# A fourth tile on GpSimd, exponentials taken from PSUM ahead of a top-16 search, and a product in two halves

## The chip, the cores and the metric

The kernel runs on one core of one Trainium2 chip. The metric is the device time of one launch in microseconds (us). The engines are named as in the profile: PE is TensorE's matrix multiply and PEld its weight load, DVE is VectorE, ACT is ScalarE, POOL is GpSimd, and SP issues most of the DMAs.

## The reference

Four transformer blocks, one after the other, act on x of 128 batches x 64 tokens x 128 channels, with a context of the same shape and a conditioning vector for each batch. All is f32. Each block has layer norms, whose scale and shift come from the conditioning, attentions with 16 heads of 8 channels, and from the second block on an MLP. The third block holds the part that matters here: a cross attention that keeps only the 16 greatest of 64 scores in each row, and takes the softmax over these.

```python
def _ln(x):
    m = x.mean(-1, keepdims=True)
    v = jnp.mean((x - m) ** 2, axis=-1, keepdims=True)
    return (x - m) * jax.lax.rsqrt(v + EPS)
...
scores = jnp.einsum('bqhd,bkhd->bhqk', q, k) / jnp.sqrt(jnp.float32(D))
top_s, top_i = jax.lax.top_k(scores, TOPK)          # TOPK = 16 of 64
attn = jax.nn.softmax(top_s, axis=-1)
vg = jnp.take_along_axis(v_bh[:, :, None, :, :], top_i[..., None], axis=3)
o = jnp.einsum('bhqk,bhqkd->bqhd', attn, vg).reshape(B, L, C)
```

There are 128 x 16 x 64 = 131,072 such rows of scores.

## The kernel before

**Chunks and lanes.** The 128 batches are cut into 16 chunks of 8 batches, which is 512 tokens: four tiles (NT = 4) of 128 tokens x 128 channels. Eight lanes work on eight chunks at once; each lane takes its next chunk when the former is nearly written out. A chunk passes through all four blocks: seven attentions, three MLPs, and twelve normal forms (ten of x, two of the context).

**The planner.** No operation is written in the order in which it is executed. Each one is recorded by `op` (L179) with an engine, a cost in ns, the tiles that it writes and reads, and a closure that issues its instructions. `Plan.run` (L347) then picks, step by step, the operation that can start earliest by these costs, over a window of 80 operations in each lane. The costs are jittered by up to 1% (`near`, L324), from the numbers in LUCK, one for each 350 steps; another LUCK gives another order. Operations with `port=True` are kept apart in the plan between DVE and POOL (L232), and a POOL operation of this kind is made to wait for the last such DVE instruction where that is near (L294). Tiles come from pools: 30 of "some" (128 x 512 f32 in SBUF), three "mm" banks, two "ps" and one "po" in PSUM.

**The normal form.** `moments` (L699) takes the sums on DVE, `normal` (L714) takes the root on POOL (L719, L720) and then, on DVE, four tensor_scalar instructions (L727), one for each tile, of which each subtracts a mean and multiplies by the root. `flip` (L688) turns the four tiles on PE (L694) into PSUM, and `modulate` (L735) multiplies by the scale (DVE, L738) and adds the shift (POOL, L739).

**Attention.** Ordinary rows go through `weigh` (L808): scores on PE (L819), exponentials on ACT straight out of PSUM (L830), the weighted sums on PE (L949), a copy (L959), a spill to DRAM (L960), the sums and their reciprocal (L977, L984), and a product on POOL (L994). The searched rows of the third block go through `weigh_rows` (L836), with queries on the partitions. Each call has two halves of 8 score rows x 64. A half is copied from PSUM by ACT (L867). On DVE, for each of the 8 rows, MAX8 finds the 8 greatest (L887), MATCH_REPLACE8 takes them out (L889), and a second MAX8 finds the next 8 (L891). One scalar_tensor_tensor (L902) then makes a mask of all scores that are not less than the sixteenth, and sums the mask into `counts`. ACT takes the exponential of the copy in place (L909), POOL multiplies it by the mask (L917), and PE turns the result (L925) for the weighted sums.

**The check at the end and the safe network.** The counts of all chunks add up in `acc[2]` (L1012), and the reciprocals and sums of the softmaxes in `acc[0]` and `acc[1]` (L1007, L1008). After the last chunk three comparisons are made, and the third of them asks for exactly sixteen in every row:

```python
    nc.vector.tensor_scalar(ok[:, 8 * NH :], acc[2], float(8 * TOPK * nchunk), None, ALU.is_equal)
...
    with tc.If(rows_ok < P):
        network(1, True)
```

`network(1, True)` is the whole network once more, with one lane, fewer buffers and `safe` set: every attention then takes `weigh_rows`, the ordinary ones subtract the row's maximum first (L870, L871), and the search takes its 16 out one by one with a second MATCH_REPLACE8, so that equal scores are told apart.

**The MLPs.** `mlp_out` (L1064) sums four products for each of the four token tiles into one PSUM bank, 16 matrix products recorded as one PE operation (L1072), and `residual` follows on DVE and POOL.

Of the kernel before, what the change touches and what calls it, by code (L numbers as in the profile page):

```python
# [10 lines left out]
AF = mybir.ActivationFunctionType  # L11
# [10 lines left out]
NT = T // P  # L22
# [2 lines left out]
COPIES = 8  # L25
MLP = 512
LANES = 8
NJ = MLP // P
LUCK = (
    47423, 97277, 61821, 98454, 87219, 72030, 46625, 79421, 30261, 36474, 64224,  # L30
    16425, 63569, 65745, 68055, 16097, 89257, 63092, 89779, 79691, 72039,
)
NSOME = 30
NQBD, NPROB, NVAL = 3, 8, 4
SCALE = 1.0 / math.sqrt(HD)
# [64 lines left out]
PE, DVE, ACT, POOL, SP, LATER = "PE", "DVE", "ACT", "POOL", "SP", "LATER"  # L100
# [31 lines left out]
class Plan:  # L132
# [43 lines left out]
        t.real, t.taken = real, True  # L176
        return t

    def op(self, engine, cost, outs, ins, give, latency=0.0, bulk=False, table=None, small=0, within=False, port=False, moves=None, rate=1.0, code=4):  # L179
        tiles = list(dict.fromkeys([*outs, *ins]))  # L180
        needs = {}
        for t in tiles:
            if t.writer is not None:
                needs[t.writer] = True
        for t in outs:
            needs.update(dict.fromkeys(t.readers))
        o = Operation(engine, cost, latency, tiles, needs, give, bulk, table, small, within, port)
        o.moves, o.rate, o.code = moves, rate, small or code
        self.count += 1
        o.serial = self.count  # L190
        o.ev = 0 if engine == PE or any(t.kind in self.PSUM for t in tiles) else 1
        for t in outs:
            t.writer, t.readers = o, []
        for t in ins:
            if t not in outs:
                t.readers.append(o)
        for t in tiles:
            t.ops.append(o)
        self.ops.append(o)
# [180 lines left out]
def kernel(ctx: ExitStack, tc: tile.TileContext, ins: dict, out: bass.AP, nchunk: int = NCHUNK):  # L380
    nc = tc.nc
# [55 lines left out]
    def prepare(plan, ready, pieces, all_of_it, vblocks, queries, pool, spills):  # L437
# [7 lines left out]
        def clear(kind, cost, give):  # L445
            t = plan.tile(lambda: None, kind)
            _, t.slot = plan.free[kind].pop()
            t.taken = True
            op(POOL, cost, [t], [], lambda: give(t.slot))
# [193 lines left out]
    def lane(n, plan, work, safe, acc, pieces, vblocks, queries, pool, spills):  # L643
# [4 lines left out]
        op = plan.op  # L648

        def of(*names):  # L650

            return [t for name in names for t in pieces.get(name, ())]

        def sb(shape, tag, bufs=1):
            name = f"{tag}{n}"
            return plan.tile(lambda: work.tile(shape, F32, tag=name, name=name, bufs=bufs), name, bufs)

        def mm(name):
            return plan.tile(lambda: mm_tile(name), "mm")

        def shared(shape, tag):

            return plan.tile(lambda: work.tile(shape, F32, tag=tag, name=tag, bufs=plan.size[tag]), tag)

        def some(shape):


            def make():
                a = pool[t.slot]
                return a.rearrange("p (a b) -> p a b", a=shape[1]) if len(shape) == 3 else (  # L670
                    a.rearrange("p (a b c) -> p a b c", a=shape[1], b=shape[2]) if len(shape) == 4 else a
                )

            t = plan.tile(make, "some")
            return t
# [9 lines left out]
            ), 3130, moves=(893, 538))  # L685
            return t

        def flip(x, name):  # L688

            p = mm(name)  # L690

            def turn():
                for t in range(NT):
                    nc.tensor.transpose(p()[:, t * P : (t + 1) * P], x()[:, t, :], ident)  # L694

            op(PE, 510, [p], [x], turn, rate=0.75, code=2 * NT)
            return p

        def moments(x, tag="parts"):  # L699
# [14 lines left out]
        def normal(x, mv, eps):  # L714

            rstd = sb([P, NT], "rstd", 2)

            def root():
                nc.gpsimd.tensor_scalar(rstd().unsqueeze(2), mv()[:, :, 2:3], 1.0 / D, eps, ALU.mult, ALU.add)  # L719
                nc.gpsimd.tensor_tensor(rstd(), rstd(), minus_half, ALU.pow)  # L720

            op(POOL, 1295, [rstd], [mv], root)
            xn = some([P, NT, D])

            def norm():
                for t in range(NT):
                    nc.vector.tensor_scalar(  # L727
                        xn()[:, t, :], x()[:, t, :], mv()[:, t, 1:2], rstd()[:, t : t + 1], ALU.subtract, ALU.mult
                    )

            op(DVE, 1180, [xn], [x, mv, rstd], norm, port=True)

            return flip(xn, "pn")

        def modulate(h, pn, key, scale, shift, c):  # L735
            made = of((key, scale), (key, shift))
# [16 lines left out]
        def attention(hq, hkv, wq, bq, wk, wv, made, topk=False):  # L753
# [82 lines left out]
            def weigh_rows(i, prs):  # L836

                quad, gp = divmod(i, 2)
                psc = plan.tile(lambda: ps_s.tile([P, 2, 2, 2, 2, S], F32, tag="ps", name="ps"), "ps")
# [20 lines left out]
                for half in range(2):  # L860
                    ex = some([P, 8, S])

                    def s8(half=half):
                        return psc().rearrange("p g u k b s -> p (g u k b) s")[:, 8 * half : 8 * half + 8]

                    if topk:
                        op(ACT, 585, [ex], [psc], lambda ex=ex, s8=s8: nc.scalar.copy(ex(), s8()))  # L867
                    else:
                        mx = sb([P, 8], "mx", 2)
                        op(DVE, 680, [mx], [psc], lambda mx=mx, s8=s8: nc.vector.tensor_reduce(mx(), s8(), AX.X, ALU.max))  # L870
                        op(DVE, 680, [ex], [psc, mx], lambda ex=ex, mx=mx, s8=s8: nc.vector.tensor_tensor(  # L871
                            ex(), s8(), mx().unsqueeze(2).to_broadcast([P, 8, S]), ALU.subtract
                        ))
                    exs.append(ex)
# [31 lines left out]
                            ), port=True)  # L906
                        ws.append(w)
                for half, ex in enumerate(exs):
                    op(ACT, 570, [ex], [ex], lambda ex=ex: nc.scalar.activation(ex(), ex(), AF.Exp, scale=SCALE), table="exp")  # L909
                    if topk:  # L910
                        w = ws[half]
                        if safe:
                            op(DVE, 690, [ex], [ex, w], lambda ex=ex, w=w: nc.vector.scalar_tensor_tensor(
                                ex(), w(), GONE, ex(), ALU.is_equal, ALU.mult
                            ))
                        else:
                            op(POOL, 1255, [ex], [ex, w], lambda ex=ex, w=w: nc.gpsimd.tensor_tensor(  # L917
                                ex(), ex(), w(), ALU.mult
                            ), port=True)
# [120 lines left out]
        def residual(py, x, gate, c, behind):  # L1040
            if isinstance(gate, str):
                op(DVE, 670, [x], [x, py], lambda: nc.vector.tensor_tensor(x(), v3(py()), x(), ALU.add))
            else:
                g = by_token(gate, 0, c, [behind])
                y = some([P, NT, D])
                op(DVE, 650, [y], [py, g], lambda: nc.vector.tensor_tensor(y(), v3(py()), g(), ALU.mult))  # L1046
                op(POOL, 1255, [x], [x, y], lambda: nc.gpsimd.tensor_tensor(x(), x(), y(), ALU.add), port=True)  # L1047
# [16 lines left out]
        def mlp_out(gs, w2, x, gate, c):  # L1064

            py = mm("py")

            def sum_up():
                for t in range(NT):
                    cols = slice(t * P, (t + 1) * P)  # L1070
                    for j in range(NJ):
                        nc.tensor.matmul(  # L1072
                            py()[:, cols], lhsT=gs[j // 2]()[:, j % 2, cols], rhs=W[w2][:, j, :], start=(j == 0), stop=(j == NJ - 1)
                        )

            op(PE, 3610, [py], [*gs, *of(w2)], sum_up, code=4 * NT * NJ)
            residual(py, x, gate, c, gs[1])

        def product(w, j, h, name, *takes):
# [6 lines left out]
        def gelu_mlp(h, w1, b1, w2, x, gate, c):  # L1086
            gs = [shared([P, NJ // 2, T], "prob") for _ in range(2)]

            def part(j):
                ph = product(w1, j, h, "ph", *([] if j else gs))  # L1090
                op(ACT, 690, [gs[j // 2]], [ph, *of("biases")], lambda: nc.scalar.activation(
                    gs[j // 2]()[:, j % 2, :], ph(), AF.Gelu_apprx_tanh, bias=bvec(b1, j)
                ), table="gelu")

            for j in range(NJ):
                part(j)
            mlp_out(gs, w2, x, gate, c)

        def swiglu_mlp(h, w1, b1, w2, x, gate, c):

            gs = [shared([P, NJ // 2, T], "prob") for _ in range(2)]

# [110 lines left out]
    def network(lanes, safe, acc=None):  # L1213
        def warm(tile, ns):
# [4 lines left out]
            while columns > 0:  # L1219
# [4 lines left out]
        slots = {"mm": 3, "ps": 2, "po": 1, "qbd": 1 if safe else NQBD, "prob": 2 if safe else NPROB,  # L1224
                 "values": 1 if safe else NVAL, "some": 10 if safe else NSOME, "spill": 1 if safe else LANES, "turned": 1 if safe else LANES}

# [32 lines left out]
    for a in acc:  # L1259
        nc.gpsimd.memset(a, 0.0)  # L1260
    network(LANES, False, acc)

# [41 lines left out]
```

## Time and profile before

| | |
|---|---|
| time, median of 3 runs | 1746.65 us (1745.8 to 1761.59) |
| the profiled execution | 1752.81 us, of which the span is 1751.0 |
| instructions in the span | 74746 |
| mean granted PE clock | 0.979 |
| busy: PE, DVE, ACT, POOL | 93%, 71%, 73%, 64% |
| normal form on DVE (L727) | 640 + 128 tiles, 262.4 us |
| searched halves: copies (L867), exponentials (L909) | 128 each, 69.7 and 80.1 us |
| search on DVE (L887, L889, L891) | 1024 rows |
| second products of the MLPs (L1072) | 3 x 512 PE instructions, 183.7 us |

The span goes from the first to the last instruction; the profiled execution's own time is 1.8 us longer. A row of the groups gives the line in the code, the engine, the operation, what is written and read with shapes, the count, then busy us and the mean ns of one, and last the idle time of the engine ahead of it with what ended it. Busy shares are averages over the span; a table by windows of 100 us shows which engine is full where.

### The profile page before, as it was taken

How to read it: one execution, taken by the hardware profiler on the slowest of the kernel's cores; microseconds unless marked ns; L12 is line 12 of the kernel's file. 1: busy time of each engine (PE TensorE's matmuls, PEld its weight loads, DVE VectorE, ACT ScalarE, POOL GpSimd, SP SyncE). 2: the span in 40 equal slices, each digit the busy share in tenths (PEclk: the TensorE clock that was granted, in tenths of full speed). 3: DMA queues.
4: the chain of work that ended last, by engine and by line, in shares of the span. 5: the costliest groups of instructions: out<-in, count | busy, mean ns of one | idle time of the engine just before them, and what ended most of it. 6: DMA issues, size and time to landing. Idle time of an engine off the chain costs nothing. (4 is left out here: it accounts for less than half of the span.)

```text
span 1751.0 us, 74746 instructions
## 1 busy us (share of the span) xinstructions
PE 1624.2 (93%) x30425; PEld 1138.2 (65%) x30425; DVE 1248.4 (71%) x6009; ACT 1272.1 (73%) x1806; POOL 1117.3 (64%) x1306
## 2 busy tenths in 40 slices
PE   8977999988899999999998999999998999999998
PEld 5655667666566566766766666677676756666665
DVE  7532545699998976694578379399989899985323
ACT  3745777867587686788687859879887668686762
POOL 8642656666566757675766485586868566666444
PEclk9988999999999999999999999999999899999999
DMA  7576655543334456545654645755454325356343
GB/s 215 164 231 178 189 169 160 158 120 112 92 118 137 115 150 193 147 137 151 171 161 129 184 130 143 211 147 158 125 175 128 98 77 177 108 153 187 118 144 99
DMA packets 296821, 260.86 MB, mean 149 GB/s; under 512 B 53196, under 2 KB 216212, under 8 KB 296468
## 3 DMA queue, kind: packets, MB, share of 16 engines
q1 hardware_dynamic: 296468, 255.99, 50.2%
q8 instruction: 242, 3.96, 1.0%
q14 instruction: 111, 0.91, 0.2%
HBM read 154.83 MB, written 79.04 MB: 134 GB/s over the span
## 5 line engine op out<-in xcount | busy, mean ns | idle before, releaser
L830 ACT ACTIVATE prob<-ps 128x1024 f32<-128x1024 f32 x384 | 376.5, 1025 | 115.1 <-PE ps L819 112.7
L949 PEld LDWEIGHTS po<-prob,vbuf 128*32 128x32 f32 x14336 | 216.1, 111 | 89.1 <-issue 41.0
L949 PE MATMUL po<-prob,vbuf 128*32 128x64 f32 x14336 | 255.9, 223 | 9.6 <-issue 5.1
L727 DVE TENSOR_SCALAR some<-x,parts,rstd 128x128 f32<-128x128 f32 x640 | 212.4, 393 | 65.0 <-POOL rstd L720 64.8
L819 PE MATMUL ps<-qbd,some 32*64 32x256 f32 x6144 | 226.8, 393 | 18.8 <-DMA qbd<-some 14.1
L917 POOL TENSOR_TENSOR some<-some,some 128x512 f32<-128x512 f32 x128 | 163.6, 1286 | 102.7 <-ACT some L909 66.8
L720 POOL TENSOR_TENSOR rstd<-rstd,minus_half 128x4 f32<-128x4 f32 x192 | 199.0, 1037 | 16.0
L889 DVE MATCH_REPLACE8 some<-m,some 128x64 f32<-128x64 f32 x1024 | 206.4, 209 | 0.3 <-issue 0.3
L1047 POOL TENSOR_TENSOR x<-x,some 128x512 f32<-128x512 f32 x112 | 142.8, 1278 | 81.4 <-DVE some L1046 51.2
L994 POOL TENSOR_TENSOR some<-some,some 128x512 f32<-128x512 f32 x112 | 143.4, 1281 | 80.1 <-DMA some<-spillrec 20.9
L959 ACT COPY some<-po 128x512 f32<-128x512 f32 x224 | 132.6, 592 | 77.9 <-PE po L949 64.9
L887 DVE MAX8 m<-some 128x8 f32<-128x64 f32 x1024 | 172.1, 209 | 15.9 <-ACT some L867 15.9
L891 DVE MAX8 m<-some 128x8 f32<-128x64 f32 x1024 | 176.9, 214 | 0.0
L819 PEld LDWEIGHTS ps<-qbd,some 32*64 32x64 f32 x6144 | 119.7, 133 | 83.8 <-issue 41.0
L792 ACT COPY vbuf<-pv 64x512 f32<-64x512 f32 x224 | 154.2, 688 | 27.4 <-PE pv L785 25.3
L739 POOL TENSOR_TENSOR some<-some,mod_L 128x512 f32<-128x512 f32 x112 | 116.7, 1044 | 84.3 <-DVE some L738 62.5
L1038 POOL TENSOR_TENSOR x<-x,some 128x512 f32<-128x512 f32 x112 | 142.9, 1278 | 42.8 <-DVE some L727 26.5
L1046 DVE TENSOR_TENSOR some<-py,some 128x512 f32<-128x512 f32 x112 | 76.1, 683 | 115.8 <-PE py L1059 63.2
L706 DVE BATCH_NORM_STATS2 parts<-x 128x6 f32<-128x256 f32 x320 | 119.7, 418 | 34.9 <-POOL x L1047 34.0
L694 PE MATMUL pn<-ident,some 128*128 128x128 f32 x768 | 122.0, 283 | 7.2 <-DVE some L727 4.7
L694 PEld LDWEIGHTS pn<-ident,some 128*128 128x128 f32 x768 | 89.2, 142 | 51.1 <-issue 16.7
L763 ACT COPY some<-pk 128x512 f32<-128x512 f32 x112 | 66.3, 593 | 57.4 <-PE pk L761 46.5
(202 smaller groups left out, 3252.4 us busy)
## 6 DMA issues: line engine op xcount, KB each, us to landing
spill<-some SPq DMA_DIRECT2D x224, 256.0 KB, 3.4
some<-gates SPq DMA_DIRECT2D x224, 256.0 KB, 3.7
qbd<-some SPq DMA_DIRECT2D x448, 64.0 KB, 2.4
some<-spill SPq DMA_DIRECT2D x112, 256.0 KB, 4.0
some<-spillrec SPq DMA_DIRECT2D x112, 256.0 KB, 4.5
some<-in_ctx_dram SPq DMA_DIRECT2D x48, 256.0 KB, 5.1
gates<-once SPq DMA_DIRECT2D x7, 1024.0 KB, 7.4
x<-in_x_dram SPq DMA_DIRECT2D x16, 256.0 KB, 4.5
```

What stands on the lines that cost most here:

```text
L694: nc.tensor.transpose(p()[:, t * P : (t + 1) * P], x()[:, t, :], ident)
L720: nc.gpsimd.tensor_tensor(rstd(), rstd(), minus_half, ALU.pow)
L727: nc.vector.tensor_scalar(xn()[:, t, :], x()[:, t, :], mv()[:, t, 1:2], rstd()[:, t : t + 1], ALU.subtract, ALU.mult)
L792: nc.scalar.copy(v4(vbuf())[rows, :, :, 0 : 2 * HD].rearrange("p m h (d b) -> p m h d b", b=2)[:, :, :, :, b], pv()[rows].rearrange("p (m ...
L819: nc.tensor.matmul(pscs[g // 2]()[b * S : (b + 1) * S, g % 2, u].rearrange("p (h q) -> p h q", h=4), lhsT=kT()[rows, cols], rhs=qbd()[rows ...
L830: op(ACT, 975, [pr], [psc], lambda pr=pr, psc=psc: nc.scalar.activation(pr().rearrange("p g u h q -> p (g u h q)"), psc().rearrange("p g u ...
L887: nc.vector.max(m1()[:, j, :], ex()[:, j, :])
L889: nc.vector.match_replace(w()[:, j, :], m1()[:, j, :], ex()[:, j, :], GONE)
L891: nc.vector.max(m2()[:, j, :], w()[:, j, :])
L917: op(POOL, 1255, [ex], [ex, w], lambda ex=ex, w=w: nc.gpsimd.tensor_tensor(ex(), ex(), w(), ALU.mult), port=True)
L949: nc.tensor.matmul(po()[32 * j : 32 * j + 32, g, u], lhsT=vbuf()[:, at : at + 32], rhs=prs[gp]()[:, gi, u, j], start=True, stop=True,)
L994: nc.gpsimd.tensor_tensor(oT().rearrange("p (t b q) -> p b t q", b=2, q=S), oS().rearrange("p (b t q) -> p b t q", b=2, q=S), rb().rearran ...
```

## The change

Three edits, and a new LUCK for the planner.

- In `normal`, DVE makes the first three tiles and POOL the fourth, with a recorded cost of 450 ns. The tile of POOL's result is the same buffer; `beside` keeps the two writers from being ordered one after the other in the plan, and `flip` waits for both. Both have `port=True`.
- In the searched attention of the first network, ACT takes the exponential as it reads PSUM, and the search, the mask and the count work on exponentials. The copy and the exponential in place are gone there. The safe network keeps copying the scores, searching these, and taking exponentials afterwards.
- `mlp_out` records its products as two operations of two token tiles each.

```diff
+ONDVE = 3
...
-    def op(self, engine, cost, outs, ins, give, latency=0.0, bulk=False, table=None, small=0, within=False, port=False, moves=None, rate=1.0, code=4):
-        tiles = list(dict.fromkeys([*outs, *ins]))
+    def op(self, engine, cost, outs, ins, give, latency=0.0, bulk=False, table=None, small=0, within=False, port=False, moves=None, rate=1.0, code=4, beside=()):
+        tiles = list(dict.fromkeys([*outs, *ins, *beside]))
         needs = {}
         for t in tiles:
-            if t.writer is not None:
+            if t.writer is not None and t not in beside:
                 needs[t.writer] = True
...
-            op(PE, 510, [p], [x], turn, rate=0.75, code=2 * NT)
+            op(PE, 510, [p], [x, *rest], turn, rate=0.75, code=2 * NT)
...
-            def norm():
-                for t in range(NT):
-                    nc.vector.tensor_scalar(
+            rest = plan.kept(True)
+
+            def norm(engine, tiles):
+                for t in tiles:
+                    engine.tensor_scalar(
                         xn()[:, t, :], x()[:, t, :], mv()[:, t, 1:2], rstd()[:, t : t + 1], ALU.subtract, ALU.mult
                     )
 
-            op(DVE, 1180, [xn], [x, mv, rstd], norm, port=True)
-
-            return flip(xn, "pn")
+            op(DVE, 885, [xn], [x, mv, rstd], lambda: norm(nc.vector, range(ONDVE)), port=True)
+            op(POOL, 450.0, [rest], [x, mv, rstd], lambda: norm(nc.gpsimd, range(ONDVE, NT)), beside=[xn], port=True)
+
+            return flip(xn, "pn", rest)
...
                     if topk:
-                        op(ACT, 585, [ex], [psc], lambda ex=ex, s8=s8: nc.scalar.copy(ex(), s8()))
+                        if safe:
+                            op(ACT, 585, [ex], [psc], lambda ex=ex, s8=s8: nc.scalar.copy(ex(), s8()))
+                        else:
+                            op(ACT, 585, [ex], [psc], lambda ex=ex, s8=s8: nc.scalar.activation(
+                                ex(), s8(), AF.Exp, scale=SCALE
+                            ), table="exp")
...
                 for half, ex in enumerate(exs):
-                    op(ACT, 570, [ex], [ex], lambda ex=ex: nc.scalar.activation(ex(), ex(), AF.Exp, scale=SCALE), table="exp")
+                    if safe or not topk:
+                        op(ACT, 570, [ex], [ex], lambda ex=ex: nc.scalar.activation(ex(), ex(), AF.Exp, scale=SCALE), table="exp")
...
-            def sum_up():
-                for t in range(NT):
+            def sum_up(half):
+                for t in (2 * half, 2 * half + 1):
...
-            op(PE, 3610, [py], [*gs, *of(w2)], sum_up, code=4 * NT * NJ)
+            for half in range(2):
+                op(PE, 1805, [py], [*gs, *of(w2)], lambda half=half: sum_up(half), code=2 * NT * NJ, within=half > 0)
```

More of the change, by code (lines that the diff above doesn't have):

```diff
@@ L27 @@
 LANES = 8
+ONDVE = 3
 NJ = MLP // P
 LUCK = (
-    47423, 97277, 61821, 98454, 87219, 72030, 46625, 79421, 30261, 36474, 64224,
-    16425, 63569, 65745, 68055, 16097, 89257, 63092, 89779, 79691, 72039,
+    47848, 24402, 28621, 90625, 6804, 13538, 44993, 48557, 31650, 48712, 55050,
+    6092, 66723, 82014, 54051, 14593, 75315, 99856, 95817, 45787, 46198,
 )
@@ L686, in load, with flip @@
             return t
-        def flip(x, name):
+        def flip(x, name, *rest):
             p = mm(name)
```

## The prediction

> **What bounds the kernel now.** I read the page's busy shares first, then the table of 100 us windows, then the groups of instructions by form, then the two lines about the normal form, and last the timeline of the final chunk, where one lane can be followed alone.
>
> ```profile
> PE 1624.2 (93%) x30425; PEld 1138.2 (65%) x30425; DVE 1248.4 (71%) x6009; ACT 1272.1 (73%) x1806; POOL 1117.3 (64%) x1306
> ...
> L727 DVE TENSOR_SCALAR some<-x,parts,rstd 128x128 f32<-128x128 f32 x640 | 212.4, 393 | 65.0 <-POOL rstd L720 64.8
> ...
> L917 POOL TENSOR_TENSOR some<-some,some 128x512 f32<-128x512 f32 x128 | 163.6, 1286 | 102.7 <-ACT some L909 66.8
> ```
>
> TensorE is busy in 93% of the span; nothing that takes work from the other engines can give back more than its idle 127 us, and the start (0 to 200 us: 14 + 18 us idle) and the last 51 us (9 us idle) don't contain the changed search at all. The rest is in the windows where VectorE searches for the sixteen greatest:
>
> ```profile
> 400.00:500.00 100.00, 84.68 (x1616) 56.97 (x1617) 97.00 (x637) 69.99 (x107) 58.45 (x62) 0.97 0.40 116
> 500.00:600.00 100.00, 92.57 (x1730) 64.69 (x1728) 92.33 (x531) 74.10 (x107) 65.98 (x73) 0.97 0.43 124
> ...
> 1200.00:1300.00 100.00, 96.34 (x2038) 68.86 (x2041) 90.56 (x497) 85.98 (x124) 68.55 (x79) 1.00 0.52 154
> ```
>
> The columns are PE, PEld, DVE, ACT, POOL, granted clock, DMA. VectorE at 90% and over is what holds TensorE there; with the windows at 1300 and 1400 TensorE idles 40.5 us in these five. The reader should also see the counts: the search (L887) has 1024 instructions, 16 chunks x 8 halves x 8 rows. The program ran its network **once**. That is a fact about the data, not only about the schedule.
>
> **The change, part by part.** The sums go against the profiled execution (1752.81 us, span 1751.0 and 1.8 around it), which is 6.2 us over the median of the runs shown, 1746.65.
>
> *The fourth tile.* 192 normal forms of four tiles each are 768 instructions, 262.4 us of DVE (212.4 + 50.0). A quarter, 65 us, leaves DVE. POOL has no 128x128 one-source row: from below, its 128x4 form (0.238 us, L719); from above, two sources at 128x64 and 128x512 (0.342 and 1.28 us), which put 128 columns at 0.48 us. I take 0.45 (one source instead of two): 192 x 0.45 = 86 us, POOL from 64% to 69%. In no window does it pass 77% (the most is 72). What stands behind it on POOL's in-order queue is the next chunk's roots, shifts and residual adds.
>
> Here a rule speaks against the word "beside". The trace has one tile at 240 ns at least, 340 as median, 1475 at most, and POOL waiting 26.5 us for it at L1038:
>
> ```profile
> L727 DVE TENSOR_SCALAR some<-x,parts,rstd x640: 240/340/1475, 16.3 to 1731.5; 128x128 f32<-128x128 f32 x160
> ...
>   POOL x L1038: 26.5, 22
>   POOL x L1033: 16.7, 20
>   POOL x L1047: 16.6, 13
> ```
>
> The 1475 is a tile plus about one 1.28 us add of POOL. The Trainium skill (SBUF — State Buffer, section Who interferes with whom) says that VectorE's two-port tensor_scalar and any GpSimd operation hold one shared pair of ports in turn, the loser blocked for the whole instruction. Four tiles undisturbed take 1.11 us in the timeline at 1701.18. If both really ran beside, the form would take max(0.83, 0.45) = 0.83 us, a gain of 0.28; by the rule 0.83 + 0.45 = 1.28, a loss of 0.17. The 1475 makes me take the rule. So the gain isn't a shorter form: it is VectorE's queue, 65 us less over the span, of which five windows of 17.5 hold 19 us.
>
> *Exponentials straight out of PSUM.* In the one pass, 128 copies (L867, 0.594 us) become exponentials and 128 exponentials (L909, 0.638) go. One that reads PSUM costs between the copy's 0.59 and 0.69 (L770, with a bias); I take 0.60. ACT: 128 x (0.594 + 0.638 - 0.60) = 81 us less, 73% to 68%. POOL's product L917 no longer waits for ACT after the search (66.8 us of its idle time); next late is the search itself. The 20 table loads ahead of L909 (25.7 us) move ahead of L867, no gain counted. The cover is TensorE's other lanes; without it the search starts a load (1.28 us) later, 20 times, 26 us.
>
> *Second sums in halves.* The same 32 instructions, 3.57 us in the chain, now twice 1.79 with room for another lane's matmul between. Nothing on TensorE changes; from -5 us (a ready scores group goes 1.8 us earlier, a few dozen times, mostly covered) to +5 (py held longer); I take 0.
>
> Sum for the one pass: up to 19 us from VectorE's windows, perhaps 5 from ACT's (TensorE's weight loads for L949 and L819 wait 25.7 us for the exponentials L830), less 9 for POOL's longer queue (a tenth of its added 86): -15. That gives 1738 on the profiled execution, **1732** against the median.
>
> **What the exponential does to the check.** The kernel keeps every score that is not less than the 16th greatest (L902), counts what it kept, and asks at L1268 for exactly 16 in each row, 8 x 16 x 16 = 2048 per partition and column; one row with 17 makes rows_ok less than 128, and L1276 then runs the whole network again with one lane in the safe form. Before, the compared numbers are raw scores; after, they are exponentials, f32 in a f32 tile. That matters because these scores are small. From the reference's inputs: scaled scores have a standard deviation of 0.052, so their exponentials lie about 1, where f32 steps are 1.19e-7 (0.6e-7 under 1), while a raw score near 0.1 has steps of 0.75e-8. There are 128 x 16 x 64 = 131,072 rows. Gaps of the 16th to the 17th exponential: median 0.0014, but ten rows lie under one step. Rounded to f32, **three rows have the 16th equal to the 17th**; summing 1 - gap/step over the ten rows expects 4.6, and with the scores shifted by 3e-8 to 1e-6 (other orders of rounding) there were 1 to 9 such rows, never none. At four expected, none at all has a chance of e^-4, 2%. Of raw scores the same sum expects 0.1 rows and the reference has none, which agrees with the single pass in the trace.
>
> A second rule bears on this: the Trainium skill (ScalarE: Activation LUTs, section ACT is a hardware spline evaluator) has exp off by up to 165 units in the last place, a smooth cubic on each segment. Smooth means that the rounding step still decides: it shifts which rows tie, not how many. With the rule or with exact exponentials I expect some four rows. No run here shows it.
>
> **The price of a second pass.** It has one lane, so latencies add. Out of the timeline from 1692.89 to 1716: the normal form from moments to shifted h, 6.3 us (1699.01 to 1705.32); queries to first scores 6.0 (1692.89 to 1698.90); scores 1.1; then 8 halves with a maximum and a subtraction on DVE out of PSUM, each as long as L738 (0.68): 10.9; exponential, transposes, copy 2.1; weighted sums and copy 1.9; from the spill through sums, reciprocal, spillrec to the broadcast back 15.7 (1699.65 to 1710.82 and the 4.5 to land); product with rb, projection, two residuals 4.6. Together 49 us. Six such are 294. The searched one has per half four groups at 0.9 us in the timeline, 1.3 with the second replacement, and 0.69: 5.9 x 8 = 47 in place of 10.9, so 85. Three MLPs, each 6.3 + 5.7 + 3.7 + 2.0 = 18, with the second products of the gated one 56. Load and store 7. A chunk is 442 us, and the next one can't begin on x before: 16 x 442 = 7070. With the first pass 1738 + 7070 = 8808, say **8800** us. If a quarter of each chunk overlaps (the context's side, the next gates) it is 7000; if waits in SP's one queue and a slower TensorE clock add 28%, 10800.
>
> **The rivals.** *A, the forecast:* a tie, second pass, 8800 (7000 to 10800). For it: the count of ties and the check in the code. Against: no row of this trace compares exponentials. *B:* every row has exactly 16, one pass, and TensorE's waits behind VectorE shrink: 1732 (1712 to 1755). It is the one on the other side: its place is L1268, its price zero, and it decides if no row ties, or if I read the count wrongly. *C:* one pass, and POOL's tile costs more than it saves: it waits in turn for VectorE's three with all that is queued behind; at 0.17 us on each of 192 forms 33 us if nothing covers it, 1785 - 6 = 1779. It decides where a form is on TensorE's path; the chain has L727 at only 1%, which is against it. *D:* one pass, all of it hidden behind TensorE: 1747.
>
> **How the numbers follow.** A 0.62, B 0.28, C 0.05, D 0.05. The tie count alone would give A more; I hold it down because it rests on the reference's rounding and my reading of the count, neither seen on this chip. A measurement of this kernel tells about 1% from no change. Faster by over 1%: two thirds of B, 0.19. Within 1%: the rest of B and D, 0.14. Slower: A and C, 0.67. The range has to hold A and most of the one-pass cases: 1712 to 10800; A's own stands above.
>
> **What would show it.** The page would have about double the instructions, L867's safe copies and the DVE maximum of L870 present, TensorE busy under a third over the whole, and slices full in the first fifth and thin after. In the first pass: no L909 for the search, DVE's normal form x576, POOL's x192 at 0.35 to 0.50. I am wrong if the span ends near 1740 with 1024 search instructions; then the ties are absent or not counted. A second pass of under 5 ms would make the latency sum wrong, not the mechanism.

## The result: 8747.5 us, and the profile after

The changed kernel takes 8747.5 us (8745.41 to 8749.01, 4 runs) against 1746.61: 4.998 times as long, 95% interval 4.971 to 5.025. The page of the changed kernel says at once what happened. These are its span, its busy shares, and its VectorE, ACT and POOL slices (each slice is 219 us):

```profile
span 8746.0 us, 213897 instructions
...
PE 7265.9 (83%) x89547; PEld 4432.1 (51%) x89547; DVE 3562.6 (41%) x15033; ACT 2997.0 (34%) x4619; POOL 2431.5 (28%) x2734
...
DVE  4796699423242424232424242323242324232423
ACT  5767777522222222222222222222222222222222
POOL 6777787511111111111111111111111111111111
```

There are 213,897 instructions where there were 74,746. Eight slices are full, as before; then 32 thin ones follow, and VectorE's digits rise to 4 about once in two slices, which is one searched attention to each chunk. The second network ran. Its start can be read to the microsecond at the conversion of the count (tile n_ok, L1285):

```profile
L1285 DVE CAST n_ok<-pok x1: 134/134/134, 1737.7 to 1737.7; 1x1 int32<-1x1 f32 x1
```

From there to the end are 8746.0 - 1737.7 = 7008 us. The table of two windows (PE, PEld, DVE, ACT, POOL, clock, DMA share, GB/s) sets the passes side by side:

```profile
0.00:1738.00 1738.00, 1612.32 (x30405) 1124.89 (x30405) 1214.55 (x5817) 1204.93 (x1675) 1268.14 (x1498) 0.98 0.52 150
1738.00:8746.00 7008.00, 5653.59 (x59142) 3307.23 (x59142) 2348.10 (x9216) 1792.06 (x2944) 1163.32 (x1237) 0.91 0.12 36
```

In the second pass DMA falls from 52% to 12%, and ACT and POOL to 26% and 17%. That is one lane whose steps wait for each other. PE looks busy, at 81%. But 3216 of its 5654 us are fillers, matrix products without use that the planner puts into long gaps (L1232); the network's own work is 38% of the second pass. Here are L1232's share of the second window (PE, PEld, clock, DMA share, GB/s), and groups after 1745 us with shapes kept apart:

```profile
1738.00:8746.00 7008.00, 3215.76 (x7430) 1427.23 (x7430) 0.91 0.12 36
...
L1232 PE MATMUL pn<-ident 128*128 128x512 f32 x1264 | 672.8, 678 | 0.0
L1232 PE MATMUL ppt<-ident 128*128 128x512 f32 x1238 | 666.9, 672 | 0.0
...
L879 DVE TENSOR_REDUCE mx<-ps 128x8 f32<-128x512 f32 x768 | 493.1, 684 | 1325.8 <-PE ps L853 1325.6
L880 DVE TENSOR_TENSOR some<-ps,mx 128x512 f32<-128x512 f32 x768 | 491.1, 681 | 0.0
...
L1004 POOL TENSOR_TENSOR some<-some,some 128x512 f32<-128x512 f32 x112 | 141.3, 1262 | 3184.1 <-DMA some<-spillrec 2513.3 <-issue 592.9 <-PE pc L695 77.9
```

The number behind the second bar is idle time ahead: POOL's product L1004 has 3184 us of it, 2513 ended by the broadcast of the reciprocals. The maxima L879, absent before, are there 768 times (16 chunks x 6 ordinary attentions x 8 halves).

### The profile page after: what moved, and what is told of

The parts are those of the page before. It is cut to its first block, busy times and chain, and to the rows that moved or that the text cites. A ratio compares the mean times of both kernels' runs of the same rounds, so it can differ in the third digit from the quotient of the medians.

```text
span 8746.0 us, 213897 instructions
## 1 busy us (share of the span) xinstructions
PE 7265.9 (83%) x89547; PEld 4432.1 (51%) x89547; DVE 3562.6 (41%) x15033; ACT 2997.0 (34%) x4619; POOL 2431.5 (28%) x2734
## 5 line engine op out<-in xcount | busy, mean ns | idle before, releaser
L1004 POOL TENSOR_TENSOR some<-some,some 128x512 f32<-128x512 f32 x224 | 285.1, 1273 | 3243.4 <-DMA some<-spillrec 2550.7
L935 PE MATMUL ppt<-ident,some 128*128 128x128 f32 x4096 | 669.8, 302 | 445.1 <-DVE some L923 222.0
L879 DVE TENSOR_REDUCE mx<-ps 128x8 f32<-128x512 f32 x768 | 493.1, 684 | 1325.8 <-PE ps L853 1325.6
L1232 PE MATMUL ppt<-ident 128*128 128x512 f32 (+24 forms) x2154 | 964.6, 580 | 0.0
L919 ACT ACTIVATE some<-some 128x512 f32<-128x512 f32 x896 | 536.3, 630 | 944.4 <-POOL some L906 415.5
L1232 PE MATMUL pn<-ident 128*128 128x512 f32 (+15 forms) x1640 | 798.2, 636 | 1.4 <-DVE n_ok L1285 1.4
L853 PE MATMUL ps<-some,qbd 32*64 32x64 f32 x32768 | 643.5, 225 | 109.7 <-DMA qbd<-some 71.5
L944 ACT COPY prob<-ppt 128x512 f32<-128x512 f32 x1024 | 577.6, 588 | 450.6 <-PE ppt L935 447.2
L853 PEld LDWEIGHTS ps<-some,qbd 32*64 32x64 f32 x32768 | 557.0, 136 | 222.0 <-DMA qbd<-some 106.2
L1232 PEld LDWEIGHTS ppt<-ident 128*128 128x128 f32 x2154 | 414.6, 210 | 362.0 <-issue 349.6
L1232 PE MATMUL py<-ident 128*128 128x512 f32 (+9 forms) x1418 | 590.9, 566 | 0.0
L1232 PEld LDWEIGHTS pn<-ident 128*128 128x128 f32 x1640 | 343.9, 220 | 372.9 <-issue 371.1
L880 DVE TENSOR_TENSOR some<-ps,mx 128x512 f32<-128x512 f32 x768 | 491.1, 681 | 0.0
```

The costliest lines, as they stand in the source:

```text
L853: nc.tensor.matmul(psc()[e * S : (e + 1) * S, gi, u, k, b], lhsT=qbd()[rows, 2 * k + e, cols], rhs=kT()[rows, cols], start=True, stop=True,)
L935: nc.tensor.transpose(ppt()[:, k * P : (k + 1) * P], ex()[:, 2 * k : 2 * k + 2, :].rearrange("p b s -> p (b s)"), ident,)
L944: nc.scalar.copy(pr8[:, 4 * half : 4 * half + 4], ppt().rearrange("p (k q) -> p k q", k=4))
L1004: nc.gpsimd.tensor_tensor(oT().rearrange("p (t b q) -> p b t q", b=2, q=S), oS().rearrange("p (b t q) -> p b t q", b=2, q=S), rb().rearran ...
L1232: nc.tensor.matmul(flat[:, :n], lhsT=ident, rhs=ident[:, 0:1].to_broadcast([P, n]), start=True, stop=True)
```

## The experiments

**Theory.** Rounded to f32, some rows have equal sixteenth and seventeenth exponentials; the count is 17, the check fails, and the safe network runs. **Rivals.** The count goes wrong on exponentials in another way; or one of the other two edits breaks the check; or the safe network only became slow by these edits. (The check's other two comparisons only ask that sums stay under 2^64 and 2^100.) Runs 1, 2, 4, 5 and the exchange of LUCK in 6 are single executions.

**1. How many partitions fail.** The branch is replaced by a row of branches whose memsets can be counted in the profile.

```diff
-    with tc.If(rows_ok < P):
-        network(1, True)
+    mark = const.tile([P, 64], F32, name="mark")
+    for k in range(12):
+        with tc.If(rows_ok < P - k):
+            nc.gpsimd.memset(mark, float(k))
```

> The changed kernel with the second network left out; in its place twelve branches, k = 0 to 11, each with one memset if fewer than 128 - k partitions passed, so that the number of memsets is the number of partitions that failed. Equal sixteenth and seventeenth exponentials: the reference's scores expect about 4 such rows, so 1 to 9 memsets, and a time near 1740 us. The rival that the count itself goes wrong for exponentials (or that the sums fail): all 12 memsets, since then nearly every partition would fail.

It took 1742.05 us, one pass. The group of its memsets:

```profile
L1290 POOL MEMSET mark<- 128x64 f32 x2 | 0.3, 151 | 0.1
```

Two: exactly 126 of 128 partitions passed. The first rival would have failed nearly all. Where about four rows are expected, two or fewer have a chance of about a quarter, so the number agrees without being close.

**2. The dose.** The searched exponential gets an eighth of the scale, so that the values crowd eight times nearer to 1; the row of branches has 64 steps.

```diff
-                                ex(), s8(), AF.Exp, scale=SCALE
+                                ex(), s8(), AF.Exp, scale=SCALE / 8
```

> The counting kernel with 64 branches, and an eighth of the scale inside the searched exponential, which changes the attention's weights: all exponentials move eight times nearer to 1, while the f32 step stays. If rounding to f32 makes the equal pairs, the reference's scores give about 29 such rows in 28 partitions (23 to 32). If the two partitions had another cause (a wrong count, a fault in one row): 2 memsets again.

```profile
L1290 POOL MEMSET mark<- 128x64 f32 x30 | 4.6, 152 | 2.9 <-POOL mark L1290 0.4
```

Thirty partitions where 28 were expected (23 to 32). The only thing changed in the values is their spacing against the f32 step, and the count follows it, so values closer than the step make the equal pairs. Together with runs 3 and 4 this settles the cause. Whether ACT's own approximation of the exponential adds or removes a pair here and there is not separated: the counts are those of f32 rounding within their scatter.

**3. The exponentials undone alone.** The fourth tile and the halves stay.

```diff
                     if topk:
-                        if safe:
-                            op(ACT, 585, [ex], [psc], ... nc.scalar.copy(ex(), s8()))
-                        else:
-                            op(ACT, 585, [ex], [psc], ... AF.Exp, scale=SCALE), table="exp")
+                        op(ACT, 585, [ex], [psc], ... nc.scalar.copy(ex(), s8()))
...
-                    if safe or not topk:
-                        op(ACT, 570, [ex], [ex], ... AF.Exp, scale=SCALE), table="exp")
+                    op(ACT, 570, [ex], [ex], ... AF.Exp, scale=SCALE), table="exp")
```

> The changed kernel with the exponentials alone undone: copy, search of raw scores, exponential in place; the fourth tile on GpSimd and the halves stay. If equal exponentials cause the second pass: one pass, 1735 to 1755 us. If the tile on GpSimd or the halves had a part in it: near 8750 us still.

1858.42 us, 1.062 of before (1.060 to 1.064): one pass, so the other two edits don't call the second network. But it isn't 1735 to 1755. That miss is taken up in 6.

**4. The exponentials alone, on the kernel before** (the reverse of the diff in 3, on the old file).

> The kernel before with the exponentials alone, its own LUCK kept. If equal exponentials cause the second pass: a first pass near 1740 and a second near 7000, together 8700 to 8750 us. If one of the other edits is needed for it: near 1745 us.

8701.86 us, with a span of 8700.1. Its count is converted at 1803.2:

```profile
L1280 DVE CAST n_ok<-pok x1: 135/135/135, 1803.2 to 1803.2; 1x1 int32<-1x1 f32 x1
```

The second pass takes 8700.1 - 1803.2 = 6897 us. One edit of three is enough to call it. The first pass, again, isn't the 1740 that I wrote.

**5. The kernel before, made to run its own safe network.**

```diff
-    with tc.If(rows_ok < P):
+    with tc.If(rows_ok < P + 1):
```

> The kernel before with the branch's bound raised by one, so that the safe network always runs after the first. If the whole loss is the safe network's latency: 8700 to 8760 us, as in the changed kernel. If a part of it comes from the tile on GpSimd within the safe network (12 forms x 16 chunks in a row, POOL's tile at 0.8 us): 20 to 60 us less than the changed kernel's 8747.

8651.9 us, with a span of 8650.1; the count is converted at 1743.1:

```profile
L1274 DVE CAST n_ok<-pok x1: 136/136/136, 1743.1 to 1743.1; 1x1 int32<-1x1 f32 x1
```

The second pass takes 6907 us. So nothing in the change had to make the safe network slow: it was always there, at this price. The changed one's is 101 us longer, 1.5%, more than I had allowed. To see which edit that is, all four tiles were put back on VectorE in the changed kernel, and its second pass read:

```diff
-            op(DVE, 885, [xn], [x, mv, rstd], lambda: norm(nc.vector, range(ONDVE)), port=True)
-            op(POOL, 450.0, [rest], [x, mv, rstd], lambda: norm(nc.gpsimd, range(ONDVE, NT)), beside=[xn], port=True)
-            return flip(xn, "pn", rest)
+            op(DVE, 1180, [xn], [x, mv, rstd], norm, port=True)
+            return flip(xn, "pn")
```

> The changed kernel with all four tiles on VectorE in both networks; exponentials, halves and LUCK stay, so the second pass is called. Only the second pass is read (from the count's conversion to the end): 7008 us in the changed kernel, 6907 in the kernel before with its branch forced. If GpSimd's tile is the 101 us between them: about 6905. If the halves are: about 7008.

8662.57 us, with a span of 8660.7:

```profile
L1282 DVE CAST n_ok<-pok x1: 133/133/133, 1781.7 to 1781.7; 1x1 int32<-1x1 f32 x1
```

The second pass takes 8660.7 - 1781.7 = 6879 us. With the tile on GpSimd it is 7008 - 6879 = 129 us longer. The kernels of 4 and 5, whose second networks are the same, differ by 10 us (6897 and 6907), so the 129 is clear of what single runs scatter; and the halves, which they lack, did not make the second pass longer.

**6. The first pass.** It has to be timed without the second. The branch is kept, but for more than 16 failing partitions:

```diff
-    with tc.If(rows_ok < P):
+    with tc.If(rows_ok < P - 16):
```

> The changed kernel, whose second network runs only if more than 16 partitions fail, so that two failing partitions no longer call it (rows with equal sixteenth and seventeenth exponentials keep both). It is the first pass alone, timed. My sum for it: 1732, 15 us under before. If GpSimd's tile at 0.8 us (not 0.45) takes back what the exponentials give: 1745 to 1750.

1746.8 us against 1747.95: 0.9998, from 0.998 to 1.0016. The first pass is neither faster nor slower. It lies where I had put a tile that takes back what the exponentials give, but the number alone doesn't show that cause. And the 1858 and 1803 us of 3 and 4? Both had a LUCK that was not found for their operations. The kernel before with the changed kernel's numbers and no other edit tests what that is worth:

```diff
 LUCK = (
-    47423, 97277, 61821, ...
+    47848, 24402, 28621, ...
```

> The kernel before with the changed kernel's LUCK and nothing else: the same instructions in another planned order. If the order alone is worth little: 1735 to 1765. If the 1858 us of the kernel with raw search and the 1803 us first pass of the one with exponentials alone are mostly a LUCK that was not found for them: 1790 to 1870.

1792.24 us, 45 more than with its own, for the same computation in another order (some fillers differ). So single edits can only be compared when each has a LUCK of its own. I looked for one in the same way for three kernels, keeping what the planner itself expected to finish earliest.

The diff in 3 with a found LUCK (GpSimd's tile and the halves):

> The changed kernel with raw search as before and a LUCK found for it: GpSimd's tile and the halves remain. If the order made the 1858 us: 1745 to 1780. If GpSimd's tile of 0.8 us costs by itself: over 1800 still.

The kernel of 3 with all four tiles on VectorE (the diff in 5), so the halves alone:

> The kernel before with the halves alone and a LUCK found for it. If the halves are worth nothing: 1745 to 1765, the rest being what one found LUCK differs from another. If they help: under 1735.

Exponentials and halves, four tiles on VectorE, one pass as in the first diff of 6:

> The changed kernel's first pass (the second is called at more than 16 failing partitions only) with all four tiles on VectorE and a LUCK found for it: exponentials and halves without GpSimd's tile. If the exponentials bring the 5 to 20 us that I counted and GpSimd's tile takes them back: 1725 to 1740. If nothing of the edits shows in a pass bound by TensorE: 1745 to 1755.

| kernel, LUCK found alike | us | of before, 95% interval |
|---|---|---|
| tile and halves | 1787.92 | 1.024, 1.021 to 1.027 |
| halves | 1782.59 | 1.021, 1.018 to 1.024 |
| exponentials and halves | 1739.35 | 0.996, 0.993 to 0.998 |

All three searches were alike. The first two times fit neither of the cases that I had written down for them. The kernels with and without the exponentials differ by 43 us; the first two are 5 us apart, too little to mean anything beside what an order is worth. Yet "halves alone" is 35 us over before, whose own LUCK is clearly a better find than mine, so each row carries an order's chance of that size. That the exponentials help a first pass is likely from this, and not shown: it would need several found orders for each kernel. The halves alone at 1783 don't show that halves cost anything either.

The last row is under the kernel before by 0.4%, which is clear of the scatter of its runs and far less than an order is worth. It gets there by letting rows with equal values keep 17 scores, so it isn't a replacement for a search that takes exactly 16.

## Why the prediction was right, and where its steps were off

- **The equal values: right.** Expected some four rows and a chance of 2% for none; two partitions failed, and at an eighth of the scale 30 where the same count from the reference gives 28. The 0.62 that I gave the case was lower than this argument alone supported, as the prediction says.
- **The price of the second pass: right to 1%, in part by luck.** 7070 was the sum, 7008 the measure. By its terms, for single stretches: a chunk 442, measured 437 on average from one searched attention to the next; an ordinary attention with its normal form 49, measured 48.6 from residual to residual (4095.28 to 4143.90); the searched one 85, measured 89.3 (4143.90 to 4233.19); the gated MLP 20 (56 less two of 18), measured 19.3 (4233.19 to 4252.51). The latencies could be read off the last chunk of the kernel before, since that lane already ran nearly alone. But the sum was made for a second network in which the tile on GpSimd costs nothing. Without that tile it takes 6879 to 6907, so the sum was 2.5% too high, and 129 us that I had not counted made up most of the difference.
- **A step that was wrong: GpSimd's tile at 0.45 us.** It measured 0.8, so POOL has 151 us more, not 86, and its fullest window of 100 us is at 86% in the kernel of one pass, where I had said that none passes 77%.

The tile's line (L730) in the kernel of one pass; min, median and max in ns:

```profile
L730 DVE TENSOR_SCALAR some<-x,parts,rstd x480: 239/343/1418, 16.3 to 1726.1; 128x128 f32<-128x128 f32 x160
...
L730 POOL TENSOR_SCALAR some<-x,parts,rstd x160: 787/797/1067, 17.4 to 1724.4; 128x128 f32<-128x128 f32 x160
```

  I interpolated between POOL's two-source rows and took something less because this has one source. But it also reads two scalars for each partition, and nothing in the trace of before had that on POOL at this width. The bounds, 0.24 and 0.48, did not hold it: I drew the upper one from an operation of another kind. What in the operation costs the time is not shown.
- **"In turn, by the rule": wrong for the tile, right for POOL's wide operations.** I took the rule of the Trainium skill (SBUF — State Buffer, section Who interferes with whom), by which VectorE in a two-port mode and GpSimd block each other for a whole instruction. First the timeline of a lone chunk in the changed kernel:

```profile
2290.96 1.01 DVE L730 TENSOR_SCALAR some<-x,parts,rstd 128x128 f32<-128x128 f32 x3 [1.44 <-POOL rstd L721]
2291.03 0.86 POOL L730 TENSOR_SCALAR some<-x,parts,rstd 128x128 f32<-128x128 f32 x1
2292.12 1.26 POOL L1043 TENSOR_TENSOR x<-x,plain_L1c 128x512 f32<-128x512 f32 x1 [0.23 <-DVE some L730]
```

  Columns: start, duration, engine. VectorE's three tiles take 1.01 where alone they take 0.86, POOL's one 0.86 where alone 0.79, and both end within 0.1 us. In turn they would need 1.65. The form is 1.01 against 1.11 with four tiles on VectorE: beside each other, at a small price. Had I priced the tile at 0.8 and in turn, I should have expected a loss of 0.5 on each form, and the timeline doesn't have it here. Now a form in the kernel of one pass that meets a POOL product of 128x512 with two sources:

```profile
255.12 1.85 DVE L730 TENSOR_SCALAR some<-x,parts,rstd 128x128 f32<-128x128 f32 x3 [1.21 <-POOL rstd L721]
...
255.06 1.27 POOL L1004 TENSOR_TENSOR some<-some,some 128x512 f32<-128x512 f32 x1
```

  The three tiles take 1.85: the first is held until the product is over. Counted over the whole traces, 63 of 768 of VectorE's tiles took over 0.6 us before, and 73 of 576 in the kernel of one pass. Every one of them overlaps a two-source POOL operation of 128x512 and ends 0.08 to 0.09 us after it. No tile without such an operation beside it took over 0.49, the 151 beside POOL's fourth tile among them. So the 1475 ns that made me take the rule was a hold of this kind, by another operation than the one that I was pricing. POOL's 26.5 us at L1038 are no evidence for the rule: that add overwrites the x that the tile reads, so the program makes it wait.
- **How often they run beside each other.** The planner makes a POOL operation with `port=True` wait for VectorE's last where that is near, the fourth tile too. In the kernel of one pass 63 of the 192 POOL tiles overlap VectorE's, in the changed kernel's second pass 144 of 192.
- **Where the second pass loses instead.** The 129 us are not a price of each form. From the sums of one normal form to the sums of the next, the two stretches of a chunk that hold an MLP and nothing else take 16.38 and 19.32 us (means of 14 chunks) with the tile on GpSimd, and 16.39 and 19.34 with four tiles on VectorE. The loss is in other stretches, and three places can be seen. First, POOL takes its work in order, and in one attention of the seven, the first of the second block, the context's tile stands ahead of the product that the lane waits for:

```profile
2276.49 0.52 SPq L1000 DMA_DIRECT2D some<-spillrec  x1
2279.94 0.86 DVE L730 TENSOR_SCALAR some<-some,seen,rstd 128x128 f32<-128x128 f32 x3 [5.17 <-DMA some<-in_ctx_dram]
2280.97 0.79 POOL L730 TENSOR_SCALAR some<-some,seen,rstd 128x128 f32<-128x128 f32 x1 [37.27 <-DVE some L730]
2281.73 1.26 POOL L1004 TENSOR_TENSOR some<-some,some 128x512 f32<-128x512 f32 x1
```

  By the median of these broadcasts, 3.7 us, the one issued at 2276.49 lands at about 2280.2 (an estimate); the product starts at 2281.73, behind a tile that had itself waited for VectorE's three. Over the 16 chunks it starts 5.2 us after the issue, and 4.3 with four tiles on VectorE: 0.9 x 16 = 14 us. In the other six attentions the two kernels differ by 0.1 us at most. Second, where the context's form follows one of x at once, at the turn from chunk to chunk, its root (1 us on POOL) stands ahead of the fourth tile of x; that stretch takes 24.4 us against 23.2, about 18 us in all. Third, in the self attention of the third block, ACT's table load comes behind the wait for VectorE's subtraction, and no longer ahead of it. Here is that place in one chunk with the tile on GpSimd, then in one with four tiles on VectorE:

```profile
3677.01 1.28 ACT L919 ACT_TABLE_LOAD   x1 [5.18 <-DVE some L880]
3678.31 1.15 ACT L919 ACTIVATE some<-some 128x512 f32<-128x512 f32 x2
...
3682.41 1.28 ACT L916 ACT_TABLE_LOAD   x1
3687.54 1.28 ACT L916 ACTIVATE some<-some 128x512 f32<-128x512 f32 x2 [3.85 <-DVE some L877]
```

  It is so in all 16 chunks, and in none of the three kernels with four tiles on VectorE; this stretch is 2.3 us longer, about 36 us in all. Why the load moved is not shown, and the remaining 60 us or so stay open. I named what stands behind the tile on POOL's queue, but gave it 9 us in the first pass and nothing in the second.
- **The first pass: 1732 forecast, 1746.8 measured, so no gain.** Of the 19 us from VectorE's windows little came. Its five fullest windows in the changed kernel are these two and three like them:

```profile
400.00:500.00 100.00, 87.93 (x1761) 60.16 (x1760) 99.47 (x662) 61.01 (x91) 61.86 (x65) 0.98 0.36 104
...
1400.00:1500.00 100.00, 97.20 (x1845) 68.34 (x1843) 96.94 (x571) 69.54 (x102) 74.08 (x82) 1.00 0.46 136
```

  VectorE is as full there as before (472 of 500 us, before 469), and TensorE idles 36.6 us, before 40.5. Over the pass the normal form takes 35 us off VectorE, not 65. The sum took a quarter of all its time, but the time in which a tile is held did not shrink with the number of tiles: 52 forms with a held tile took 106 us before, and 57 take 107 in the kernel of one pass. Only the others gave something back, 156 us for 140 of them before and 120 for 135 after. ACT's saving came as counted: the exponential from PSUM is 599 ns (0.60 was taken) and the 128 at L909 are gone. Where it went in a pass whose order was drawn anew can't be separated from that order, which alone is worth 45 us.
- **Two signs that I had wrong.** TensorE was to be busy for under a third of the whole; it was 83%. Without the fillers it would still be 49%, so they are only a part of it. The instructions were to double, and are 2.9 times as many: the safe network computes all its scores in the small form of `weigh_rows`, and has 7430 fillers.

## What to carry to other kernels

A kernel with a checked fast path has a second time hidden in it; for each edit that touches the checked values, count from the inputs how often the check will fail, before counting microseconds. A monotonic function keeps the order of real numbers, but after rounding it merges those that lie closer than its output's step, and values crowded about 1 merge far sooner than small scores about 0. Before a share of an engine's time is moved to another engine, ask how much of it is waiting that will not shrink with the work. Where an order is searched for a program, edit and order have to be separated, each edit with a search of its own, and more than one found order if the edit is worth less than an order is.

## What the runs showed of the hardware

A GpSimd tensor_scalar over 128x128 f32 with two operands for each partition takes 0.79 us at least, where VectorE's takes 0.24 at least and 0.34 as a rule. It runs beside VectorE's of the same kind with each slowed by a tenth to a fifth (1.01 for 0.86, 0.86 for 0.79). VectorE's tile meets a two-source GpSimd operation of 128x512 otherwise: 73 tiles in the kernel of one pass took 0.61 to 1.42 us, each held until that operation was over. An ACT table load takes 1.28 us, and is hidden or not by whether it stands ahead of a wait or behind it.
